# A transformer block on one core: the units without a dense product, and the row sums of the softmax, are put at another place in each chunk

## The chip, the cores and the metric

The kernel runs on one core of a Trainium2 chip. The metric is the device time of one execution in microseconds (us); three runs of the kernel before gave 5135.66, 5136.07 and 5133.8, median 5135.66. The profile shown below was taken of another execution, which took 5133.48 us.

## The reference, cut to what matters

The input x has 4 sequences of 2048 tokens with 512 features, float32. Each is normalised; then the result is x plus attention plus a feed-forward part:

```
xn  = layernorm(x)
qkv = xn @ qkv_w.T + qkv_b            # 16 heads of 32
att = softmax(q k^T / sqrt(32)) v     # over all 2048 keys
a   = att @ proj_w.T + proj_b
idx = top_2(xn[:, 0, :] @ Wr + br)    # two of 8 experts for a whole sequence
h   = gelu(xn @ W1[idx] + b1[idx])    # exact gelu
f   = (h @ W2[idx] + b2[idx]).sum(over the two) / 2
out = x + a + f
```

All matrix products are float32, except one small product described below.

## The kernel before, in words

**Units and chunks.** The attention is one long sequence of 1024 units. A unit is one tile of 128 keys against 512 queries of four heads (a group of heads). 16 units (kt = 0 to 15, NT = 16) make a chunk: one sequence b, one group of heads g, one block of queries qc. 4 chunks make a group, 4 groups a sequence, and there are 64 chunks, numbered here 0 to 63. The program is written out in one loop over U, the number of the unit, and every engine works through its own instructions in the order in which this loop issues them.

**What one unit issues.** On TensorE (PE): four small bf16 products that put minus the row maximum into four PSUM tiles (`shift`, L536, tiles s), the scores themselves on top (`score`, L544), and four score products of the unit 22 places ahead, of which only the maximum is wanted (`score_max`, L526, tiles m). ScalarE (ACT) takes the exponentials of the four s tiles (L656, into p). VectorE (DVE) takes the maxima of the four m tiles (L662). GpSimd (POOL) adds p to a running sum psum of the chunk (`add_weights`, L573 for the first and L575 for the others; not in the last chunk). Then, in even units, PE multiplies the p of the two units before with the values (`weigh`, L556, tile acc), which DVE adds up (L565). In odd units PE does one dense product of 32 matmul records (`product`, L395): a piece of a projection (kps, qps, vps, prps) or of the feed-forward part (hps, ops). So a pair of units does two sets of scores, one `weigh` and one dense product.

**Once per chunk.** After a chunk has ended, its psum is summed over the keys by a product with ones (`add_keys`, L581, tile keys), here in unit kt = 4 of the next chunk; ACT copies the result to SBUF (sums, L593). DVE takes the reciprocal in four parts in units 5, 7, 9 and 11 (L674), POOL multiplies in unit 12 (`divide`, L627) and SP stores the result two units later. In unit 13 PE transposes the maxima of a chunk ahead (`turn_maxima`, L618, tile mt), which DVE copies (L621); POOL has prepared them with five small instructions in unit 10 (L608, L610). In the last chunk there is no psum: `add_last` sums the p of two units by ones on PE, two units after them (16 matmul records).

**PSUM.** All these tiles come from one pool of eight banks (`ps`). A unit takes eight of them for its s and m tiles, and one more for acc or for the dense product; keys and mt each take one as well. A new tile goes into the bank that came free the longest ago, so a tile waits for the reader of an older tile.

**Who decides what a gap is.** `Plan` lays 496 dense products on 534 odd places (22 before unit 0, 512 after it), so 38 places have none: the gaps. Some products have fixed places (`fixed`: the k, q and v of the next group, L52 to L63); the feed-forward part and the output projection fill the rest in order. `rests` (L104 to L107) names the places where a gap is wanted, at kt = 13 of chosen chunks; 8 more are left over at the end of the list. A gap isn't put directly after the last w1 product of an expert, because the gelu stands there. Of the 38 gaps 29 lie at kt = 13, five at 15, two at 1 and two at 11: chunks 62 and 63 have four each (kt 1, 11, 13, 15), chunk 61 has two.

**Other things that a step below touches.** `root` (L342 to L347) takes the square root for the next sequence's normalisation in unit 1 of chunks 8, 24 and 40; its first instruction is a DVE operation on 128x16 numbers in SBUF (L343, sd<-mv). The buffers of p are four (`p_pool`): the exponentials of unit U + 4 wait until POOL has added unit U. The 32 gelus of ACT bring their tables with them. At the very end (L741 to L767) stand the last `weigh`, the last `add_last`, the projections of the last two blocks of queries and the stores.

Of the kernel before, what the change touches and what calls it, by code (L numbers as in the profile page):

```python
# [17 lines left out]
P = 128  # L18
# [12 lines left out]
class Plan:  # L31
# [6 lines left out]
    def __init__(self, B, DC, NCH, NT, TPC):  # L38
        self.per_group = NCH * NT
        self.per_seq = DC * self.per_group  # L40
        self.units = B * self.per_seq
        self.lead = NT + AHEAD
        self.items = {}
        self.extra = {}
        self.uses = []
        self.first_load = {}
        slots = list(range(-self.lead, 0)) + list(range(1, self.units, 2))

        fixed = {}
        for t in range(NT):  # L50
            fixed[slots[t]] = ("v", 0, t)
        for G in range(1, B * DC):  # L52
            b, g = divmod(G, DC)
            for c in range(NCH):
                if g:
                    at = [(G - 1) * self.per_group + 2 * (6 + 4 * c) + 1]
                    todo = [("k", b, g, c), ("q", b, g, c)]
                else:
                    at = [(G - 2) * self.per_group + 2 * (27 + (2 + TPC) * c) + 1]
                    todo = [("k", b, g, c), ("q", b, g, c)]  # L60
                    todo += [("v", b, c * TPC + i) for i in range(TPC)]
                for n, item in enumerate(todo):
                    fixed[at[0] + 2 * n] = item  # L63
        v_stored = {}
        for s, item in fixed.items():
            if item[0] == "v":
                v_stored[item[1], item[2] // TPC] = s + 3
        for b in range(B):
            for g in range(DC):
                for c in range(NCH):  # L70
                    self.first_load["v", (b, g, c)] = v_stored[b, c]
        for b in range(1, B):
            q1 = (b - 1) * self.per_seq + self.per_group
            q2 = q1 + self.per_group
            for n in range(NT):
                self.extra.setdefault(q1 + 2 * (16 + n) + 1, []).append(("stats", b, n))
                at = q2 + 2 * (1 + n + n // TPC) + 1
                self.extra.setdefault(at, []).append(("normal", b, n))
                self.extra.setdefault(at + 2, []).append(("turn", b, n))
            self.extra.setdefault(q2 + 1, []).append(("root", b, 0))  # L80
            for c in range(NCH):
                self.first_load[("xf", (b, c))] = self.first_load[("xq", (b, c))] = (
                    q2 + 2 * (2 + (TPC + 1) * c + TPC - 1) + 1 + 2
                )

        ffn = []
        for b in range(B):
            t0 = slots[0] if b == 0 else self.first_load[("xf", (b, 0))] + WARN
            for c in range(NCH):
                part = [("w1", b, c, k, f) for k in range(TOP_K) for f in range(DC)]  # L90
                part += [("w2", b, c, k, i) for k in range(TOP_K) for i in range(TPC)]
                ffn.append((t0, part))
        proj = []
        for b in range(B):
            for qc in range(NCH):
                if b == B - 1 and qc >= NCH - 2:
                    continue
                done = (b + 1) * self.per_seq - self.per_group + NT * (qc + 1) + 14
                self.first_load[("xl", ("at", b, qc))] = done + 1
                proj.append((done + 1 + WARN, [("proj", b, qc, i) for i in range(TPC)]))  # L100


        todo = len(fixed) + sum(len(p) for _, p in ffn + proj)
        spare = len(slots) - todo - 2 * TPC  # L104
        free = [s for s in slots if s > 0 and s not in fixed]
        rests = [s for s in free if s % NT == 13]
        rests = {rests[n * len(rests) // spare] for n in range(min(spare, len(rests)))}  # L107
        current, before, owed = [], None, 0
        for s in slots:
            if s in fixed:  # L110
                self.items[s] = [fixed.pop(s)]
                before = None
                continue
            curve = before is not None and before[0] == "w1" and before[4] == DC - 1
            before = None
            owed += s in rests
            if owed and not curve:
                owed -= 1
                continue
            if not current:  # L120
                for queue in (proj, ffn):
                    if queue and queue[0][0] <= s:
                        current = queue.pop(0)[1]
                        break
            if current:
                before = current.pop(0)
                self.items[s] = [before]
        assert not fixed and not proj and not ffn and not current, (proj, ffn, current)

        for s in slots:  # L130
            for it in self.items.get(s, []):
                for tag, key in self.needs(it):
                    self.uses.append((s, tag, key))
            for kind, b, n in self.extra.get(s, []):
                if kind in ("stats", "normal"):
                    self.uses.append((s, "xl", (kind, b, n // TPC)))
                elif kind == "turn":
                    self.uses.append((s, "xq", ("stage", b, n // TPC)))
        self.uses.append((self.units, "wb", ("proj",)))
        for u in range(2, self.units + 1, 2):  # L140
            kt, G = (u - 2) % NT, (u - 2) // self.per_group
            self.uses.append((u, "v", (*divmod(G, DC), kt // TPC)))
        self.uses.sort(key=lambda e: e[0])
        for s, tag, key in self.uses:
            if tag == "prow":
                self.first_load[tag, key] = 0
# [40 lines left out]
def block_kernel(  # L187
# [17 lines left out]
    B, N, D = x.shape  # L205
    E = Wr.shape[1]
    DC = D // P
    NT = N // P
    NCH = N // CH
    TPC = CH // P  # L210
    SCALE = float(HD) ** -0.5
    PSUM = bass.MemoryType.PSUM
    plan = Plan(B, DC, NCH, NT, TPC)
# [11 lines left out]
    def bank(name):  # L225
        return ps.tile([P, CH], F32, tag="bank", name=name)
# [284 lines left out]
    mx, negm, sacc, psums, sums, pT = {}, {}, {}, {}, {}, {}  # L511
    curves, waiting, ends = {}, {}, []
# [64 lines left out]
    def add_keys(where, ps, weights, again):  # L577

        for n, t in enumerate(weights):
            for j in range(GH):  # L580
                nc.tensor.matmul(  # L581
                    ps[rows_of(j), :], ones, t[:, j, :],
                    start=(n == 0), stop=(n == len(weights) - 1),
                )
        if again:
            nc.vector.tensor_tensor(sums[where], ps, sums[where], ALU.add)
        else:
            last = where == place(plan.units - 1)[:3]
            sums[where] = pair.tile(
                [P, CH], F32, tag="vrow" if last else "sums", bufs=2 if last else 1,  # L590
                name="sums_%d_%d_%d" % where,
            )
            nc.scalar.activation(sums[where], ps, AF.Identity)  # L593

    def add_last(u):
        add_keys(
            place(u)[:3], bank(f"keys_{u}"), [pT[u], pT[u + 1]], u > plan.units - NT
        )
# [37 lines left out]
    for U in range(-LEAD, plan.units):  # L636
        second = U >= 0
        first_pass = U + LEAD if U + LEAD < plan.units else None
        chunk, kt = divmod(U, NT)
        b, g, qc, _ = place(U) if second else (0, 0, 0, 0)  # L640
# [16 lines left out]
        curve = curves.pop(U, None)  # L657
# [6 lines left out]
        if first_pass is not None and last % NT == NT - 1:  # L664
            where, n = place(last)[:3], last // NT
# [3 lines left out]
        if last % NT == 0 and 0 < last <= plan.units:  # L669
            pending[0]()  # L670
        before = place(U - NT)[:3] if U >= NT else None
        if before is not None and kt in (5, 7, 9, 11):
            q = ts((kt - 5) // 2, P)
            nc.vector.reciprocal(sums[before][:, q], sums[before][:, q])  # L674
        if before is not None and kt == 12:
            divide(before)
            later(U + 2, lambda w=before: nc.sync.dma_start(
                att_dram[w[0], w[2]][:, w[1], :], att[w]))
# [6 lines left out]
        if second and U % 2 == 0:  # L685
            if U >= 2:
                weigh(U - 2)
            if U - 2 >= plan.units - NT:
                add_last(U - 2)
            if kt == 4 and before is not None:  # L690
                add_keys(before, bank("keys_%d_%d_%d" % before), [psums[before]], False)
        for step, sb, n in plan.extra.get(U, []):
            if step == "stats":
                if n == 0:
# [6 lines left out]
            else:  # L701
                c, i = divmod(n, TPC)
# [21 lines left out]
        for n, c in ((16, NCH - 1), (1, NCH - 2)):  # L724
            if U == plan.units - n:
# [7 lines left out]
                n = DC - 1 if c == NCH - 1 else DC  # L733
# [4 lines left out]
    U = plan.units  # L738
# [72 lines left out]
```

## Time and profile before

| | |
|---|---|
| median of 3 runs | 5135.66 us (5133.8 to 5136.07) |
| the profiled execution, its own time | 5133.48 us |
| its span, first to last instruction | 5131.6 us |
| PE busy | 5054.0 us (98%) |
| POOL busy | 4534.6 us (88%) |
| DVE busy | 3449.0 us (67%) |
| ACT busy | 2516.2 us (49%) |
| mean granted TensorE clock | 0.998 |

The time of an execution is 1.9 us above its span. Lines in the profile begin with the line of the kernel and the engine; then come the operation, the tile written and the tiles read (buffer numbers left out), how often, and in the table of groups the busy time, the mean of one in ns and the idle time ahead of it with what ended it. A line of the timeline has its start, its length, and in brackets the idle time of that engine before it with its releaser. A PE that the page calls busy isn't always at work: the records of matmuls that wait are drawn longer. The distance from the first shift product (L536) of a unit to that of the next is the length of the unit, and shows such waits.

Unit 0 starts at 160.1 us, chunk 62 at 4955.3, chunk 63 at 5016.3; the first product of the end (L746) starts at 5091.4.

### The profile page before, as it was taken

How to read it: one execution, taken by the hardware profiler on the slowest of the kernel's cores; microseconds unless marked ns; L12 is line 12 of the kernel's file. 1: busy time of each engine (PE TensorE's matmuls, PEld its weight loads, DVE VectorE, ACT ScalarE, POOL GpSimd, SP SyncE). 2: the span in 40 equal slices, each digit the busy share in tenths (PEclk: the TensorE clock that was granted, in tenths of full speed). 3: DMA queues.
4: the chain of work that ended last, by engine and by line, in shares of the span. 5: the costliest groups of instructions: out<-in, count | busy, mean ns of one | idle time of the engine just before them, and what ended most of it. 6: DMA issues, size and time to landing. Idle time of an engine off the chain costs nothing.

```text
span 5131.6 us, 108175 instructions
## 1 busy us (share of the span) xinstructions
PE 5054.0 (98%) x46020; PEld 1776.4 (35%) x46020; DVE 3449.0 (67%) x5495; ACT 2516.2 (49%) x4571; POOL 4534.6 (88%) x1430
## 2 busy tenths in 40 slices
PE   8999999999999999999999999999999999999998
PEld 2333333333333333333333333333333333333333
DVE  5666676766766667666766767766667666666672
ACT  1455545554544545554445454555444454555543
POOL 0699898989999999999999999989999999999992
PEclk9999999999999999999999999999999999999999
DMA  4211112201122112221121221221112211021112
GB/s 165 69 62 51 46 65 89 102 30 38 67 85 69 65 65 80 72 81 44 48 93 46 79 85 54 85 85 59 40 56 89 78 63 59 18 75 34 40 43 78
DMA packets 220675, 340.20 MB, mean 66 GB/s; under 512 B 14364, under 2 KB 129052, under 8 KB 205984
## 3 DMA queue, kind: packets, MB, share of 16 engines
q1 hardware_dynamic: 220192, 333.28, 19.2%
q8 instruction: 361, 5.91, 0.5%
q14 instruction: 122, 1.00, 0.1%
HBM read 249.61 MB, written 83.62 MB: 65 GB/s over the span
## 4 chain that ended last, share of the span: by engine, by line
PE 95%; POOL 2%; ACT 1%; DVE 0%; issue 0%; DMA 0%; SPq 0%; ACTq 0%; POOLq 0%
PE acc L556 18%; PE m L526 17%; PE s L544 17%; PE ops L395 9%; PE hps L395 9%; PE s L536 7%; PE kps L395 4%; PE vps L395 4%; PE qps L395 4%; PE prps L395 4%; POOL psum L575 2%; PE keys L581 1%; ACT L656 1%; PE xt L365 1%; ACT p L656 1%; PE mt L618 0%
## 5 line engine op out<-in xcount | busy, mean ns | idle before, releaser
L575 POOL TENSOR_TENSOR psum<-psum,p 128x2048 f32<-128x2048 f32 x882 | 4008.6, 4545 | 217.3 <-ACT p L656 182.1
L662 DVE TENSOR_REDUCE mx<-m 128x1 f32<-128x512 f32 x4096 | 2542.9, 683 | 1057.5 <-PE m L526 1056.9
L656 ACT ACTIVATE p<-s 128x512 f32<-128x512 f32 x4096 | 2118.1, 602 | 1797.3 <-PE m L526 1717.9
L544 PE MATMUL s<-qT,kT 32*128 32x512 f32 x8192 | 1924.0, 589 | 0.0
L526 PE MATMUL m<-kT,qT 32*128 32x512 f32 x8192 | 1908.4, 590 | 2.7 <-DMA wk<-in_qkv_wT_dram 1.5
L526 PEld LDWEIGHTS m<-kT,qT 32*128 32x128 f32 x8192 | 929.1, 184 | 325.3 <-issue 242.3
L556 PE MATMUL acc<-p,v 128*32 128x512 f32 x8192 | 990.0, 599 | 38.5 <-ACT p L656 38.5
L544 PEld LDWEIGHTS s<-qT,kT 32*128 32x128 f32 x8192 | 765.6, 186 | 31.0 <-issue 12.8
L556 PEld LDWEIGHTS acc<-p,v 128*32 128x32 f32 x8192 | 215.3, 109 | 738.5 <-ACT p L656 428.6
L395 PE MATMUL hps<-xf,w 128*32 128x512 f32 x4096 | 466.0, 595 | 0.2 <-ACT p L656 0.2
L395 PE MATMUL ops<-wb_w,h 128*32 128x512 f32 x4096 | 466.0, 595 | 0.2 <-ACT p L656 0.2
L536 PE MATMUL s<-negm,ones_b 32*128 32x512 bf16 x4096 | 421.4, 385 | 5.3 <-ACT p L656 3.5
L565 DVE TENSOR_TENSOR sacc<-acc,sacc 128x512 f32<-128x512 f32 x448 | 309.9, 692 | 154.7 <-PE acc L556 154.7
L536 PEld LDWEIGHTS <-ones_b 32*128 32x128 bf16 x4096 | 108.6, 91 | 842.3 <-issue 835.2
L573 POOL TENSOR_TENSOR psum<-p,p 128x2048 f32<-128x2048 f32 x63 | 286.1, 4541 | 117.6 <-ACT p L656 117.6
L407 ACT ACTIVATE h<-hps,b 128x512 f32<-128x512 f32 x115 | 79.0, 687 | 353.6 <-PE hps L395 353.6
L674 DVE RECIPROCAL sums<-sums 128x128 f32<-128x128 f32 x252 | 237.3, 942 | 0.7 <-ACT sums L593 0.7
L395 PE MATMUL vps<-wb_v,xq 128*32 128x512 f32 x2048 | 233.0, 595 | 2.3 <-issue 2.0
L395 PEld LDWEIGHTS ops<-wb_w,h 128*32 128x32 f32 x4096 | 120.0, 109 | 317.6 <-issue 229.8
L395 PEld LDWEIGHTS hps<-xf,w 128*32 128x32 f32 x4096 | 120.0, 109 | 317.1 <-issue 232.1
L395 PE MATMUL kps<-xq,wk 128*32 128x512 f32 x1920 | 218.4, 595 | 1.0 <-ACT p L656 0.2
L395 PE MATMUL qps<-xq,wq 128*32 128x512 f32 x1920 | 218.4, 595 | 0.1
(89 smaller groups left out, 1710.8 us busy)
## 6 DMA issues: line engine op xcount, KB each, us to landing
xq<-xn_dram SPq DMA_DIRECT2D x64, 1024.0 KB, 5.7
w<-in_W_dram SPq DMA_DIRECT2D x128, 256.0 KB, 3.1
xn_dram<-xq_stage SPq DMA_DIRECT2D x16, 1024.0 KB, 7.1
v_dram<-v SPq DMA_DIRECT2D x64, 256.0 KB, 2.4
xf<-xn_dram SPq DMA_DIRECT2D x16, 1024.0 KB, 6.1
v<-v_dram SPq DMA_DIRECT2D x64, 256.0 KB, 4.0
row<-in_x_dram SPq DMA_DIRECT2D x64, 256.0 KB, 5.9
part_dram<-row SPq DMA_DIRECT2D x64, 256.0 KB, 2.1
```

Source lines behind the costliest of these rows:

```text
L395: nc.tensor.matmul(pp[rows_of(j), :], lhsT[:, rows_of(j)], rhs, start=(first and n == 0), stop=(last and n == len(terms) - 1),)
L407: nc.scalar.activation(dst, src, AF.Identity, bias=col)
L526: nc.tensor.matmul(t, qT[b, g, qc][r, ts(i, P)], kT[b, g, kc][r, :], start=True, stop=True)
L536: nc.tensor.matmul(tiles[j], ones_b[r, :], negm[b, g, qc][r, :], start=True, stop=False)
L544: nc.tensor.matmul(tiles[j], kT[b, g, kt // TPC][r, ts(kt % TPC, P)], qT[b, g, qc][r, :], start=False, stop=True,)
L556: nc.tensor.matmul(acc[r, :], held["v", (b, g, kt // TPC)][:, (kt + n) % TPC, r], pT[u + n][:, j, :], start=(n == 0), stop=(n == 1),)
L565: nc.vector.tensor_tensor(t, acc, t, ALU.add)
L573: nc.gpsimd.tensor_tensor(psums[b, g, qc], pT[u - 1], pT[u], ALU.add)
L575: nc.gpsimd.tensor_tensor(psums[b, g, qc], psums[b, g, qc], pT[u], ALU.add)
L656: nc.scalar.activation(pT[U][:, j, :], tiles[j], AF.Exp, scale=SCALE)
L662: nc.vector.tensor_reduce(dst, t, AX.X, ALU.max, negate=True)
L674: nc.vector.reciprocal(sums[before][:, q], sums[before][:, q])
```

## The change

It does five things.

1. The wanted places of gaps are kt = 5 (not 13), spread evenly over the chunks with a running share, and only 4 places (not 8) are left over at the end. There are still 38 gaps: 34 at kt = 5 of chunks 1 to 62, and in chunk 63 kt = 1, 3, 13 and 15. The change calls this filling a third of the gaps at the end: chunks 61 to 63 have five gaps instead of ten.
2. In a chunk with a gap at kt = 5 the product of the ended chunk with ones (`add_keys`) is issued in unit 5 instead of 4; the reciprocals follow in units 7, 9, 11 and 13, `divide` in 14. In the 29 other chunks, the last one among them, nothing of this moves.
3. The fixed k and q products move by one odd place (from 13 and 15, 5 and 7, to 15 and 1, 7 and 9), so that place 5 is free.
4. In the last sequence the feed-forward part of the last two blocks of tokens is done in the other order; the output projection of a block may start two units later than before.
5. In the last chunk an `add_last`, which stands two units after the first of its two units, is issued one unit later still where that later unit is a gap.

The instructions of PE are the same in number (25,316 matmul instructions in both programs); SP has two DMAs more (the output projection falls between the pieces of a feed-forward part twice more, so one weight tile of 1 MB is loaded again twice).

```
-                    at = [(G - 1) * self.per_group + 2 * (6 + 4 * c) + 1]
+                    at = [(G - 1) * self.per_group + 2 * (7 + 4 * c) + 1]
...
-            for c in range(NCH):
+            order = list(range(NCH))
+            if b == B - 1:
+                order[NCH - 2 :] = order[: NCH - 3 : -1]
+            for c in order:
...
-                done = (b + 1) * self.per_seq - self.per_group + NT * (qc + 1) + 14
+                done = (b + 1) * self.per_seq - self.per_group + NT * (qc + 1) + 16
...
-        spare = len(slots) - todo - 2 * TPC
+        spare = len(slots) - todo - 4
         free = [s for s in slots if s > 0 and s not in fixed]
-        rests = [s for s in free if s % NT == 13]
-        rests = {rests[n * len(rests) // spare] for n in range(min(spare, len(rests)))}
+        rests = [s for s in free if s % NT == 5]
+        share = spare / len(rests)
...
-            owed += s in rests
-            if owed and not curve:
-                owed -= 1
-                continue
+            if s in rests:
+                owed += share
+                if owed > 0 and not curve:
+                    owed -= 1
+                    continue
...
+        self.keys_at = {}
+        for s in range(NT, self.units, NT):
+            ends = s + NT == self.units
+            self.keys_at[s // NT - 1] = 5 if s + 5 not in self.items and not ends else 4
...
-        if before is not None and kt in (5, 7, 9, 11):
-            q = ts((kt - 5) // 2, P)
+        keys = plan.keys_at.get(chunk - 1, 4)
+        part = (kt - keys - 1) // 2 if keys == 4 else (kt - keys - 2) // 2
+        if before is not None and kt % 2 and 0 <= part < TPC:
+            q = ts(part, P)
             nc.vector.reciprocal(sums[before][:, q], sums[before][:, q])
-        if before is not None and kt == 12:
+        if before is not None and kt == (12 if keys == 4 else 14):
             divide(before)
...
-            if U - 2 >= plan.units - NT:
-                add_last(U - 2)
-            if kt == 4 and before is not None:
-                add_keys(before, bank("keys_%d_%d_%d" % before), [psums[before]], False)
+        for u in (U - 2, U - 3):
+            late = u + 3 < plan.units and u + 3 not in plan.items
+            if u % 2 == 0 and u >= plan.units - NT and late == (u == U - 3):
+                add_last(u)
+        if before is not None and kt == keys:
+            add_keys(before, bank("keys_%d_%d_%d" % before), [psums[before]], False)
```

## The prediction on record

> **What bounds the kernel now.** I read the table of engines first, then the chain of waits, then the timeline of single units, each engine by itself, and last the waits of ACT at the end.
>
> ```profile
> PE 5054.0 (98%) x46020; PEld 1776.4 (35%) x46020; DVE 3449.0 (67%) x5495; ACT 2516.2 (49%) x4571; POOL 4534.6 (88%) x1430
> ...
> PE 95%; POOL 2%; ACT 1%; DVE 0%; issue 0%; DMA 0%; SPq 0%; ACTq 0%; POOLq 0%
> ```
>
> PE is the bound, and the chain runs on it for 95%; POOL has 2%, in chunks 61 and 62. So a change pays only by shortening PE's work or the waits between its products. The instructions of PE stay the same in number, so the whole answer is in the waits. They are seen in unit lengths, from first shift product (L536) to first shift product. The timeline of PE, a gap at unit 13 of chunk 10 and the pair after it:
>
> ```profile
> 1007.19 0.39 PE L536 MATMUL s<-negm,ones_b 32*128 32x512 bf16 x4
> ...
> 1009.24 0.40 PE L618 MATMUL mt<-ident_b,spread 128*128 128x128 bf16 x4
> 1009.67 0.86 PE L536 MATMUL s<-negm,ones_b 32*128 32x512 bf16 x4
> ...
> 1010.65 0.70 PE L526 MATMUL m<-kT,qT 32*128 32x512 f32 x2
> ...
> 1012.57 1.92 PE L556 MATMUL acc<-p,v 128*32 128x512 f32 x16
> 1014.42 0.39 PE L536 MATMUL s<-negm,ones_b 32*128 32x512 bf16 x4
> ...
> 1020.04 0.40 PE L536 MATMUL s<-negm,ones_b 32*128 32x512 bf16 x4
> ...
> 1023.94 0.39 PE L536 MATMUL s<-negm,ones_b 32*128 32x512 bf16 x4
> ```
>
> The normal pair takes 1023.94 - 1014.42 = 9.52: an odd unit with a product 5.61, an even one 3.90. The gap pair takes 14.42 - 7.19 = 7.23. Its work is only 1.99 (a bare odd unit, read at kt = 15) + 0.44 (mt: 6.05 against 5.61 in units 13 with a product) + 3.90 = 6.33; 0.90 is a wait. What it waits for is on ACT and DVE:
>
> ```profile
> 1008.53 2.06 ACT L656 ACTIVATE p<-s 128x512 f32<-128x512 f32 x4 [1.83 <-PE m L526]
> 1011.38 1.09 ACT L656 ACTIVATE p<-s 128x512 f32<-128x512 f32 x2 [0.78 <-PE s L544]
> ```
>
> The four exponentials end at 1010.59, 3.40 after the unit's start, and at 1010.65, or 3.46, the first m product of the next unit starts, into the bank just freed; what is queued behind it on PE waits as well. From there it is 1.92 to acc and 1.85 more to the next unit. ACT is then idle for 0.78.
>
> [...] A unit's s and m tiles fill all eight, so a unit without a product must wait for its predecessor's readers; the 0.90 above agrees. [...] it repeats here, 7.23 in 21 of the 27 gaps at kt = 13 up to chunk 61. [...]
>
> ```profile
> 783.42 4.28 DVE L343 TENSOR_SCALAR sd<-mv 128x16 f32<-128x16 f32 x1
> ...
> 2027.24 0.61 DVE L343 TENSOR_SCALAR sd<-mv 128x16 f32<-128x16 f32 x1
> ```
>
> In chunk 8 POOL's add had begun at 783.14 and ended at 787.67; in chunk 24 POOL was late and began at 2027.76.
>
> **The change part by part.**
>
> *Gaps up to chunk 61, before.* The 21 gap pairs above wait 0.90 each = 18.9. In six (chunks 6, 7, 22, 23, 38, 39) a stats step of DVE stands before the copy of mt, whose bank the next unit wants; the pair takes 7.94: 6 x 1.61 = 9.7. Three at kt = 15 wait 1.33 each, 4.0, one of them in chunk 62. Up to chunk 61 that is 31.3.
>
> *The same, after: 33 gaps at unit 5 with keys inside.* What keys costs on PE is seen in unit 4 now:
>
> ```profile
> 1042.85 1.04 PE L581 MATMUL keys<-psum,ones 128*32 128x512 f32 x8
> 1043.82 0.40 PE L536 MATMUL s<-negm,ones_b 32*128 32x512 bf16 x4
> ...
> 1043.95 0.60 ACT L593 ACTIVATE sums<-keys 128x512 f32<-128x512 f32 x1 [1.48 <-PE keys L581]
> ```
>
> 0.97 to the next unit; since unit 4 is 4.76 against 3.90, its net work is 0.86. In a gap it starts 2.04 after the unit's start, where mt starts now (1009.24), and the next shift comes at 3.0 instead of 2.48. The next m product still can't start before the exponentials end, at 3.46; from there 1.92 + 1.85 as above: again 7.23, but with 1.99 + 0.86 + 3.90 = 6.75 of work in it. The wait falls from 0.90 to 0.48. The 0.70 of the m product after a wait, against 0.59 otherwise, may go: then 0.38. I take 0.45; bounds 0.18 (only the change-over between kinds of products, 0.97 + 2.04 - 1.99 - 0.86 = 0.16) and 1.34 (keys not hidden at all). ACT's copy of keys fits: the exponentials end at 3.41, the next begin at 4.19, the copy takes 0.60. The stats step no longer matters, since ACT frees that bank. In chunks 8, 10, 24, 25 and 42 a transposition (0.59) lies in the gap too, and fills it: wait 0.1. Sum 28 x 0.45 + 5 x 0.1 = 13.1; saved 31.3 - 13.1 = 18.2. mt in unit 13 is now uncovered, 0.44; it is counted as work on both sides.
>
> *The lock.* In chunk 24 POOL's last add of the chunk before must end over 7.7 after its start for DVE to come first (8.2 now). Chunk 23 loses its gap but gets three additions of rows (L680, 1.3 each) late; I work out about 7.6. It costs nothing to 3.2, what unit 2 of chunk 8 waits now; I take 0.5.
>
> *Chunks 62, 63 and the end.* Before:
>
> ```profile
> 5017.96 2.06 ACT L656 ACTIVATE p<-s 128x512 f32<-128x512 f32 x4 [2.38 <-POOL psum L575]
> 5023.66 2.06 ACT L656 ACTIVATE p<-s 128x512 f32<-128x512 f32 x4 [3.64 <-POOL psum L575]
> ...
> 5019.11 18.36 POOL L575 TENSOR_TENSOR psum<-psum,p 128x2048 f32<-128x2048 f32 x4
> ```
>
> Four gaps make chunk 62 61.0 long, while POOL needs 15 x 4.6 for its adds; it ends at 5037.5, 21.2 into chunk 63, and the exponentials wait for p buffers. Work in chunk 62: 5 x 3.90 + 4 x 5.61 + 2.0 (gap) + 0.86 up to unit 9, then without m tiles (0.85 less each) 3 x 3.05 + 3 x 1.1 + 0.44: 57.7, wait 3.3. From chunk 63 to the first end product 75.1, with work 3.05 (unit 0) + 4 x 1.1 (gaps) + 10 x 4.77 (scores and a product, or `weigh` and `add_last`) + 5.6 (unit 4, with keys) = 60.75, and 3.6 for the last `weigh` and `add_last`: 64.35, wait 10.75. Together 14.05. After, chunk 62 has one gap and 69.1 of work; POOL starts its first add 7.4 into it and needs 15 x 4.6 + 1.3 (divide) + 1.3 (five small ones) = 71.6, so it ends about 10 to 11 into chunk 63. There unit 3's exponentials wait 1.0 for it, the gap at unit 1 costs 1.1, the gaps at 3, 13 and 15 are filled by `add_last` (1.72), the last exponential 0.5; with chunk 62's own gap 0.45: 3.05. Saved 11.0.
>
> *At nothing.* The moves with one answer: the k and q products only change places with others of the same 3.64. Reciprocals in 13 instead of 5: DVE there has 2.48 of maxima to 3.85, 0.94, 0.4 for mt, 0.8 with stats, all under the unit's 6.05; beyond that the next unit's m waits. `divide` and its store two units later: POOL is 1 to 2 us later after a gap (7.23 against two adds of 4.6), its adds then start 7 to 11 after their unit's start; the four p buffers allow about 15, then exponentials wait. The store stands ahead of all later loads on SP; POOL has two units (9.5) for it, and loads are issued 8 units ahead. The projection starts four units after its load, as now. Two more loads of 1 MB (6.9 each), 8 units (38 us) ahead. The 31 waits of 1.23 after gelus stay.
>
> *Sum.* 18.2 - 0.5 + 11.0 = 28.7 on a span of 5131.6: 5102.9. That execution took 5133.48, 2.2 under the median; I subtract from the median: 5135.66 - 28.7 = 5107.
>
> **Rivals.** (1) The forecast, with 0.38 to 0.48 per gap, lock 0 to 3.2, end within 3: 5102 to 5113. (2) Gaps filled nearly wholly, 0.18: 28 x 0.27 = 8 better, 5099. For it: keys delays the next unit until the banks are free but one. Against: that one, the last exponential at 3.41. (3) POOL still sets the pace at the end: its adds end 18 rather than 10 into chunk 63, so some 7 of the 11 stay, and the lock strikes in chunk 24, 2.7: 5117. For: POOL is the chain there now. Against: one gap instead of four. (4) Keys not hidden: 29 x 0.86 = 25 worse, 5132, no change. For: the wait is a chain through ACT, and keys adds a tile to it. Against: PE stands still while ACT works. (5) Slower: the copy of keys stands on ACT between the exponentials of units 5 and 6 and pushes the latter back, on top of (4): (0.86 + 0.60) x 34 = 50, 5157. It turns the sign from 28.7 / 34 = 0.84 per gap. For: ACT is in order. Against: 0.78 idle for 0.60, and the trace has psum ready 4 to 11 after a chunk's start, keys at 23. That the gaps don't move can't be: the plan is explicit.
>
> **Numbers.** Chances: (1) 0.60, (2) 0.13, (3) 0.16, (4) 0.06, (5) 0.05. A measurement can tell about 0.2% (10 us) from no change: faster 0.89, same 0.06, slower 0.05. Range 5097 to 5121, which leaves out (4), (5) and the tails.
>
> **What would show it.** A gap pair at kt 5 of 7.1 to 7.25, unit 4 there 3.90, gap chunks 74.3 (74.7 now), no difference by stats; L343 about 4.3 in chunks 8 and 40; chunk 63 near 63, its exponentials waiting for POOL under 3 in all. Wrong if the pairs take 8, if keys waits for psum, or if ACT waits for POOL in middle chunks.

## The result, and the profile after

The changed kernel takes 5114.66 us, the median of 6 runs (5110.6 to 5116.07); the kernel before 5135.05 us (5133.78 to 5136.07, 6 runs). The ratio is 0.996, with a 95% interval of 0.9947 to 0.9973: 20.4 us faster, where 28.7 were forecast. The profiled execution took 5115.77 us with a span of 5114.0.

The lines named below moved by 8: the shift product is L544 now, the exponentials L664, keys L589, the copy of keys L601, POOL's adds L581 and L583, the DVE operation of `root` L351. The table of engines, and the engines of the chain:

```profile
PE 5037.9 (99%) x46020; PEld 1763.7 (34%) x46020; DVE 3448.0 (67%) x5491; ACT 2515.2 (49%) x4576; POOL 4534.9 (89%) x1430
...
PE 2%; DVE 0%; ACT 0%; issue 0%
```

PE has the same 46020 records and is drawn 16.1 busy us shorter; its waits shrank, not its work. The chain could be followed back for 2% of the span only, so it is of no use here, and unit lengths must tell the rest. A gap at unit 5 of chunk 11, in the timeline of PE (units 4, 5, 6 and 7 begin with the shift lines):

```profile
1033.04 0.39 PE L544 MATMUL s<-negm,ones_b 32*128 32x512 bf16 x4
...
1036.94 0.39 PE L544 MATMUL s<-negm,ones_b 32*128 32x512 bf16 x4
...
1039.02 1.07 PE L589 MATMUL keys<-psum,ones 128*32 128x512 f32 x8
1040.02 0.40 PE L544 MATMUL s<-negm,ones_b 32*128 32x512 bf16 x4
...
1040.40 0.70 PE L534 MATMUL m<-kT,qT 32*128 32x512 f32 x2
...
1042.31 1.92 PE L564 MATMUL acc<-p,v 128*32 128x512 f32 x16
1044.17 0.40 PE L544 MATMUL s<-negm,ones_b 32*128 32x512 bf16 x4
```

Unit 4 takes 36.94 - 33.04 = 3.90 without keys; the gap pair takes 44.17 - 36.94 = 7.23 with keys in it. The first m product starts 40.40 - 36.94 = 3.46 after the gap's start, as before, and 1.91 and 1.86 follow. ACT in the same place:

```profile
1038.28 2.06 ACT L664 ACTIVATE p<-s 128x512 f32<-128x512 f32 x4 [1.83 <-PE m L534]
1040.20 0.63 ACT L601 ACTIVATE sums<-keys 128x512 f32<-128x512 f32 x1
1041.36 2.14 ACT L664 ACTIVATE p<-s 128x512 f32<-128x512 f32 x4 [0.53 <-PE s L552]
```

The copy stands exactly in ACT's idle stretch and still leaves 0.53 of it. The end, chunk 63 from 5007.08 on, on ACT and then on POOL:

```profile
5013.90 2.07 ACT L664 ACTIVATE p<-s 128x512 f32<-128x512 f32 x4 [0.38 <-POOL psum L583]
5018.51 2.06 ACT L664 ACTIVATE p<-s 128x512 f32<-128x512 f32 x4 [2.54 <-POOL psum L583]
```

```profile
5008.08 1.28 POOL L635 TENSOR_TENSOR att<-sacc,sums 128x512 f32<-128x512 f32 x1
5009.32 9.15 POOL L583 TENSOR_TENSOR psum<-psum,p 128x2048 f32<-128x2048 f32 x2
```

POOL's last add ends at 5018.47, 11.4 into chunk 63 instead of 21.2, and ACT waits 2.92 for it.

The other half of the result is in `root`, where an instruction of DVE lasts until an add of POOL that has begun before it is done (in chunk 8 of the changed kernel 779.62 to 783.90, beside POOL's 779.34 to 783.87); the prediction calls this the lock. L343 before, L351 now, each of the three executions during the attention (shortest, median and longest in ns):

```profile
L343 DVE TENSOR_SCALAR sd<-mv x3: 606/4278/4298, 783.4 to 3266.4; 128x16 f32<-128x16 f32 x3
```

```profile
L351 DVE TENSOR_SCALAR sd<-mv x3: 4277/4278/4279, 779.6 to 3247.8; 128x16 f32<-128x16 f32 x3
```

All three now take 4.28; the short one, in chunk 24, is gone. There POOL's first add began at 2016.42, and DVE's operation, at 2016.71, came second. And PE, in chunk 8 (timeline, then windows of 1 us: length, busy shares of PE, PEld, DVE, ACT and POOL, granted clock, share and rate of DMA):

```profile
784.78 1.12 PE L534 MATMUL m<-kT,qT 32*128 32x512 f32 x2 [1.20 <-ACT h L415]
786.69 3.26 PE L564 MATMUL acc<-p,v 128*32 128x512 f32 x16 [0.79 <-ACT p L664]
```

```profile
784.00:785.00 1.00, 0.22 (x1) 0.22 (x2) 0.82 (x3) 0.98 (x3) 0.40 (x2) 1.00 0.02 4
785.00:786.00 1.00, 0.90 (x2) 0.07 (x1) 1.00 (x2) 1.00 (x1) 0.08 (x1) 1.00 0.00 0
786.00:787.00 1.00, 0.31 (x4) 0.16 (x8) 0.76 (x2) 0.99 (x3) 0.00 (x0) 1.00 0.00 0
787.00:788.00 1.00, 1.00 (x9) 0.22 (x5) 0.00 (x0) 1.00 (x3) 0.00 (x0) 0.56 0.00 0
788.00:789.00 1.00, 1.00 (x12) 0.21 (x4) 0.00 (x0) 0.10 (x1) 0.82 (x1) 0.50 0.00 0
789.00:790.00 1.00, 1.00 (x12) 0.12 (x8) 0.00 (x0) 0.00 (x0) 1.00 (x1) 0.50 0.00 0
790.00:791.00 1.00, 1.00 (x12) 0.67 (x12) 0.69 (x1) 0.00 (x0) 1.00 (x1) 0.73 0.00 0
```

The sixteen acc products take 3.26 instead of 1.92: after the wait PE's clock was granted at half for 3.41 us. That happened after each of the three executions of L351, and in the kernel before only after the one in chunk 40. (The kernel before has one more such fall, in chunk 63 at 5024.2, which the changed one has not.) A mean clock of 0.998 hides it.

### The profile page after: what moved, and what is told of

The parts are those of the page before. It is cut to its first block, busy times and chain, and to the rows that moved or that the text cites. A ratio compares the mean times of both kernels' runs of the same rounds, so it can differ in the third digit from the quotient of the medians.

```text
span 5114.0 us, 108163 instructions
## 1 busy us (share of the span) xinstructions
PE 5037.9 (99%) x46020; PEld 1763.7 (34%) x46020; DVE 3448.0 (67%) x5491; ACT 2515.2 (49%) x4576; POOL 4534.9 (89%) x1430
## 5 line engine op out<-in xcount | busy, mean ns | idle before, releaser
L583 POOL TENSOR_TENSOR psum<-psum,p 128x2048 f32<-128x2048 f32 x882 | 4008.1, 4544 | 193.3 <-ACT p L664 152.7
L664 ACT ACTIVATE p<-s 128x512 f32<-128x512 f32 x4096 | 2117.1, 603 | 1817.2 <-PE m L534 1729.7
L544 PE MATMUL s<-negm,ones_b 32*128 32x512 bf16 x4096 | 404.8, 385 | 2.0 <-ACT p L664 1.8
L544 PEld LDWEIGHTS <-ones_b 32*128 32x128 bf16 x4096 | 103.0, 91 | 857.5 <-issue 857.5
L581 POOL TENSOR_TENSOR psum<-p,p 128x2048 f32<-128x2048 f32 x63 | 286.0, 4540 | 119.4 <-ACT p L664 119.4
```

The costliest lines, as they stand in the source:

```text
L544: nc.tensor.matmul(tiles[j], ones_b[r, :], negm[b, g, qc][r, :], start=True, stop=False)
L581: nc.gpsimd.tensor_tensor(psums[b, g, qc], pT[u - 1], pT[u], ALU.add)
L583: nc.gpsimd.tensor_tensor(psums[b, g, qc], psums[b, g, qc], pT[u], ALU.add)
L664: nc.scalar.activation(pT[U][:, j, :], tiles[j], AF.Exp, scale=SCALE)
```

## The experiments

In each comparison "wait" is the length of a unit less its work, with the prediction's prices of work. The theory to be tested (A): a gap pair is as long as its chain of exponentials, 7.23, whatever small work lies in it, so keys is paid for by time that was idle; and the lock in `root` took back a part of that. Rivals: the place of the gaps rather than keys brought the gain, or the end of the program did (C); or the lock's stalls only show a delay that would be there anyway (B).

### e1_root_on_act_after: the changed kernel without the DVE operation

The small constant is added by ACT inside the square root, so the DVE operation is gone and nothing can be locked there.

```
+    eps = const.tile([P, 1], F32, name="eps")
+    nc.gpsimd.memset(eps, EPS)
-        nc.vector.tensor_scalar(sd[:np_, a:z], mv[:np_, a:z, 1], EPS, None, ALU.add)
-        nc.scalar.activation(sd[:np_, a:z], sd[:np_, a:z], AF.Sqrt)
+        nc.scalar.activation(sd[:np_, a:z], mv[:np_, a:z, 1], AF.Sqrt, bias=eps[:np_])
```

> The changed kernel with one thing taken away: in root the small DVE addition of epsilon on 128x16 (sd<-mv) is gone, ScalarE adds it as the bias of its square root. Theory A (the shortfall against the forecast is the lock): DVE's small operation waited 4.3 us behind GpSimd's add in chunks 8, 24 and 40, PE stood idle and ran at half clock for 3.4 us afterwards; unit 2 of those chunks waits 4.5, 4.2 and 4.9 us now and will wait under 0.5 us each, so some 13 us less than the changed kernel: 5101 us. Rival B (the two table loads of 1.28 us each around the square root make the wait, the lock lies beside them): unit 2 still waits 3 us or more, 5111 us or above.

Measured: 5104.73 us (5102.71 to 5105.05, 5 runs), ratio to the kernel before 0.9941 (0.9927 to 0.9954); the changed kernel stands at 0.996, so this is about 10 us less. ACT in chunk 8:

```profile
779.05 1.28 ACT L353 ACT_TABLE_LOAD   x1
780.35 0.31 ACT L353 ACTIVATE sd<-mv,eps 128x16 f32<-128x16 f32 x1
...
782.57 1.28 ACT L665 ACT_TABLE_LOAD   x1 [0.50 <-PE m L535]
```

```profile
784.51 1.92 PE L565 MATMUL acc<-p,v 128*32 128x512 f32 x16 [1.16 <-ACT p L665]
```

The waits of units 2 and 3 in chunks 8, 24 and 40 fall from 13.9 in all to 3.7, 1.23 in each; under 0.5 was expected, without the table loads of 1.28 on ACT that stay. No half clock is left before the end of the program. 13.9 - 3.7 = 10.2 is about what the times show. A holds in the main, B falls. This is the fastest version in the study.

### e2_root_on_act_before: the same edit on the kernel before

```
-        nc.vector.tensor_scalar(sd[:np_, a:z], mv[:np_, a:z, 1], EPS, None, ALU.add)
-        nc.scalar.activation(sd[:np_, a:z], sd[:np_, a:z], AF.Sqrt)
+        nc.scalar.activation(sd[:np_, a:z], mv[:np_, a:z, 1], AF.Sqrt, bias=eps[:np_])
```

> The kernel before with the same edit. Theory A: there the lock struck only in chunks 8 and 40 (3.2 and 2.9 us beyond the gelu's 1.2), so about 6 us less: 5129 us, and the difference between the two kernels without the lock is about 28 us, near the forecast of 28.7. Rival B: no change, 5135 us.

Measured: 5131.44 us (13 runs) beside 5135.84, ratio 0.9993 (0.9985 to 1.0002), an interval that touches no change. The profile gives the size: the same units fall from 8.7 to 5.0, 3.7 us, of which 1.66 is the half clock in chunk 40. So the lock and its clock cost 3.7 before and 10.2 after: 6.5 us of the change's gain were lost there. Without them the change brings 5131.44 - 5104.73 = 26.7, where about 28 was expected. The 1.66 may not belong to the lock: in chunk 40 a wait of 2.56 stays without it, and only the fall of the clock is gone.

### e3_keys_in_4: the gaps stay at unit 5, keys goes back to unit 4

```
-            self.keys_at[s // NT - 1] = 5 if s + 5 not in self.items and not ends else 4
+            self.keys_at[s // NT - 1] = 4
```

> The changed kernel with the sums over keys always in unit 4, so that the 34 gaps at unit 5 are empty; reciprocals and division follow at their old units. Theory A (the gap pair is timed by the last exponential and takes 7.23 us whatever lies in it, up to 0.48 us more): the pair still takes 7.2 us, unit 4 goes from 3.90 to 4.76, so about 0.86 x 29 and a little for the five gaps with a transposition: 27 us more than the changed kernel, 5142 us. Rival C (keys is not hidden in the gap, the gain comes from the end and from where the gaps lie): within 5 us of the changed kernel.

Measured: 5144.92 us (5143.69 to 5147.76, 13 runs), ratio 1.002 (1.0012 to 1.0028): 30 us above the changed kernel and slower than the kernel before. A gap of this kernel in the timeline of PE:

```profile
1042.76 1.04 PE L589 MATMUL keys<-psum,ones 128*32 128x512 f32 x8
1043.73 0.40 PE L544 MATMUL s<-negm,ones_b 32*128 32x512 bf16 x4
...
1045.72 1.09 PE L544 MATMUL s<-negm,ones_b 32*128 32x512 bf16 x4
...
1050.95 0.40 PE L544 MATMUL s<-negm,ones_b 32*128 32x512 bf16 x4
```

The pair is 50.95 - 43.73 = 7.22 with nothing in it; unit 4 pays its 0.86 again. 34 x 0.86 = 29.2; the five pairs with a transposition take 8.22 instead of 7.67, 2.8 more; the half clock struck once instead of three times, 3.3 less. That makes 28.7, and the profiles are 28.8 apart. So the gain is keys, not the place of the gaps; C falls for this part.

### e4_keys_twice: the product of keys is computed twice in a gap

```
+            ps_ = bank("keys_%d_%d_%d" % before)
+            if keys == 5:
+                for j in range(GH):
+                    nc.tensor.matmul(
+                        ps_[rows_of(j), :], ones, psums[before][:, j, :], start=True, stop=True
+                    )
-            add_keys(before, bank("keys_%d_%d_%d" % before), [psums[before]], False)
+            add_keys(before, ps_, [psums[before]], False)
```

> The changed kernel with the product of keys computed twice in the 33 or 34 gaps at unit 5, the second result kept. Theory A: of the 0.86 us more per gap 0.32 us fill the wait that is left (0.48 less the 0.16 of change-over), so the pair goes from 7.23 to 7.77 us and the kernel is 28 x 0.54 + 5 x 0.75 = 19 us slower, 5134 us. If nothing of the wait can be filled: 29 us slower, 5144 us. If the wait were longer than the unit lengths show: under 10 us slower.

Measured: 5131.96 us (5131.04 to 5134.39, 12 runs), ratio 0.9995 (0.9986 to 1.0003), 17.3 above the changed kernel.

```profile
1038.98 0.39 PE L544 MATMUL s<-negm,ones_b 32*128 32x512 bf16 x4
...
1041.06 1.07 PE L706 MATMUL keys<-psum,ones 128*32 128x512 f32 x8
1041.92 1.07 PE L589 MATMUL keys<-psum,ones 128*32 128x512 f32 x8
1042.92 0.39 PE L544 MATMUL s<-negm,ones_b 32*128 32x512 bf16 x4
...
1046.82 0.39 PE L544 MATMUL s<-negm,ones_b 32*128 32x512 bf16 x4
```

The pair is 46.82 - 38.98 = 7.84: of the second 0.86 only 0.25 hides, 0.61 shows. 29 x 0.61 and 0.75 in each of the five gaps with a transposition make 21.4; in this profile the half clock struck once instead of three times, 3.3 less, and unit 0 starts 2.5 earlier: 15.6, as far as the two profiles are apart. Unit 6 now has its plain 3.90, and the wait that stays, 0.23, lies in unit 5: it is the floor of a gap.

### e6_gaps_in_13: the gaps of the changed kernel put back at 13

The number of gaps up to chunk 62 and the end stay as in the changed kernel, and keys is in unit 4.

```
-        rests = [s for s in free if s % NT == 5]
+        rests = [s for s in free if s % NT == 13]
...
-            self.keys_at[s // NT - 1] = 5 if s + 5 not in self.items and not ends else 4
+            self.keys_at[s // NT - 1] = 4
```

> The changed kernel with its 34 gaps at kt = 13 instead of 5 and the sums over keys always in unit 4: the same end of the program, the same number of gaps, but the transposition of the maxima in the gap as in the kernel before. Theory A: a gap chunk takes 74.7 instead of 74.26 us, three gaps with a stats step 0.7 more, the five gaps with a turned block no longer gain: 34 x 0.43 + 3 x 0.7 = 17 us slower than the changed kernel, 5131 us; so of the gain two thirds is the content of the gaps and the rest, some 4 us net of the lock, the end. Rival C (the end makes the gain): within 5 us of the changed kernel.

Measured: 5127.22 us (5126.56 to 5129.85, 20 runs), ratio 0.9986 (0.998 to 0.9993). The gap pairs are 7.23 with mt (0.44) in them, save three beside stats (7.94), three with a transposition (7.74) and one of 7.51. Between this and the changed kernel lie 12.6 us, between this and the kernel before some 7 us. The expected 17 is there, but not alone: the gaps up to chunk 61 wait 31.9 against 14.9 in the changed kernel, 17.0 more, and the end takes 1.4 more; the units of `root` wait 4.7 less, since the clock fell once instead of three times and in chunk 24 DVE came first. By its profile the end saves 10.0 against the kernel before (177.2 from chunk 62 on, with three dense products of 3.62 more in it, against 176.3), and the units before chunk 62 wait 3.4 longer. So keys in the gap are worth some 17 us, the end 10 to 11, and `root` takes part of it back.

### e7_sums_by_dve: DVE copies keys in the chunks with a gap

```
-            nc.scalar.activation(sums[where], ps, AF.Identity)
+            if plan.keys_at.get(where[0] * 16 + where[1] * 4 + where[2], 4) == 5:
+                nc.vector.tensor_copy(sums[where], ps)
+            else:
+                nc.scalar.activation(sums[where], ps, AF.Identity)
```

> The changed kernel with the copy of keys out of PSUM on VectorE instead of ScalarE where the keys lie in a gap. If ScalarE's copy cost PE something in a gap (the rival of the forecast: it pushes the next exponentials back), this is faster. Theory A: ScalarE has 0.78 us idle there and the copy 0.60, so nothing is to be gained; VectorE is at its maxima to 3.85 us after the unit's start and frees the bank at about 4.5, 0.2 to 0.3 us later than the next product wants it, and 0.7 to 0.9 later in the four gaps with a stats step: 6 to 10 us slower, 5121 to 5125 us.

Measured: 5120.35 us (5118.73 to 5121.9, 7 runs), ratio 0.9971 (0.996 to 0.9982), 5.7 above the changed kernel. DVE in a gap (unit 5 starts at 1036.32):

```profile
1037.68 2.48 DVE L673 TENSOR_REDUCE mx<-m 128x1 f32<-128x512 f32 x4 [0.54 <-PE m L534]
1040.08 0.68 DVE L602 COPY sums<-keys 128x512 f32<-128x512 f32 x1
1040.93 2.48 DVE L673 TENSOR_REDUCE mx<-m 128x1 f32<-128x512 f32 x4 [0.17 <-PE m L534]
```

Behind four maxima the copy ends 4.44 after the gap's start; ACT's ended at 3.89. The pair grows from 7.23 to 7.41, and 34 x 0.18 = 6.1. No cost of the copy is seen on ACT, and on DVE it has one: of the two, ACT's idle stretch is the better place, the reverse of rival (5).

### e8_scores_first: the last 0.25

In the lock-free kernel, unit 6 behind a gap does its four score products ahead of the four m products, so that they don't queue behind the one that waits.

```
+        split_order = kt == 6 and plan.keys_at.get(chunk - 1, 4) == 5
+        if split_order:
+            score(U, range(GH), tiles)
         for h in range(2):
-            if second:
+            if second and not split_order:
```

> Two edits on the changed kernel: the lock taken away as in the other run, and in unit 6 after a gap the four score products with their exponentials stand ahead of the four whose maxima are wanted, so that the products that wait for the bank of the last exponential come 0.86 us later and no longer wait. Theory A: the pair falls from 7.23 to about 6.9 us (6.75 of work and 0.16 of change-over), 28 x 0.32 = 9 us, on top of 13 us for the lock: 5093 us. If the wait comes back elsewhere (VectorE gets its first m tile 0.86 us later and the next unit waits for it): no better than without the lock alone, 5101 us.

Measured: 5108.42 us (5108.06 to 5109.73, 5 runs), ratio 0.9948 (0.9935 to 0.9962): not the 5093 of the theory, nor a gain over e1. The timeline of PE:

```profile
1032.22 0.39 PE L545 MATMUL s<-negm,ones_b 32*128 32x512 bf16 x4
...
1035.30 0.39 PE L545 MATMUL s<-negm,ones_b 32*128 32x512 bf16 x4
...
1039.20 0.40 PE L545 MATMUL s<-negm,ones_b 32*128 32x512 bf16 x4
...
1041.63 3.64 PE L404 MATMUL kps<-xq,wk 128*32 128x512 f32 x32
```

```profile
1037.45 2.48 DVE L674 TENSOR_REDUCE mx<-m 128x1 f32<-128x512 f32 x4 [1.38 <-PE m L535]
1039.85 0.68 DVE L574 TENSOR_TENSOR sacc<-acc,sacc 128x512 f32<-128x512 f32 x1
1040.56 2.48 DVE L674 TENSOR_REDUCE mx<-m 128x1 f32<-128x512 f32 x4
```

The pair falls to 39.20 - 32.22 = 6.98, as the theory wanted. But the maxima start 2.15 after unit 6, against 1.54 in the changed kernel, the addition of acc stands behind them, and the maxima of unit 7 begin only when DVE has done both; PE's m products in unit 7 wait for their banks, and the dense product starts 2.43 after that unit's start instead of 1.99. Unit 7 waits 0.40, where 0.25 was saved: 34 x 0.15 = 5.1, and the two profiles stand 5.3 apart from unit 0 on. The times alone, whose intervals overlap, would not tell the two kernels apart. The wait was given back by the next engine.

### e5_add_last_not_late: the last part of the change undone

```
-            late = u + 3 < plan.units and u + 3 not in plan.items
+            late = False
```

> The changed kernel with add_last always two units after its first unit, so that the gaps of the last chunk at 3, 13 and 15 are empty. Theory A: PE waits for the exponentials of the gap units instead, about 1 us each at 13 and 15: the stretch from the start of chunk 63 to the first product of the end grows by 1 to 3 us. If add_last in the gaps gives nothing: no change of that stretch.

Measured: one run, 5116.61 us. By the profile, the stretch from the start of chunk 63 to the first product of the end takes 67.5 against 66.5 in the changed kernel, 0.9 more before rounding and just under the 1 to 3 expected; from chunk 62's start to the end it is 5114.8 - 4938.3 = 176.5 against 175.9: 0.6 us. So by this single profile, moving `add_last` into the gaps of chunk 63 is worth half a microsecond to one. The rest of the gain at the end probably lies in having one gap instead of four in chunk 62; that is not shown, since neither this nor the other order of the feed-forward part was tried alone.

## Why the prediction was right, and where it was not

The time lies in the range, and in the forecast's mechanism; it is 7.7 above the number. In the profiled spans 17.6 were saved, not 28.7. Step by step:

**Gaps up to chunk 61: right.** The pair was worked out as 7.23 and is 7.23; the wait is 0.48 where 0.45 was taken. One small term was too low: a gap with a transposition waits 0.33, not 0.1, since a floor of 0.23 stays (e4), a little above the 0.16 of the change-over. The 33 gaps wait 14.9 in all, forecast 13.1: 1.8 missed. The stats steps make no difference, as forecast. The contents of a gap side by side:

| in the gap | kernel | work of the pair | pair | wait |
|---|---|---|---|---|
| nothing | e3 | 5.89 | 7.22 | 1.33 |
| mt | before, e6 | 6.33 | 7.23 | 0.90 |
| keys | changed | 6.75 | 7.23 | 0.48 |
| keys and a transposition | changed | 7.34 | 7.67 | 0.33 |
| keys twice | e4 | 7.61 | 7.84 | 0.23 |
| a transposition alone | e3 | 6.48 | 8.22 | 1.74 |

The last row is not timed by the exponentials: in chunk 10 of e3, DVE copies the transposed tile only from 971.09 to 971.72, after a reciprocal of 0.94, and two m products, released by it, start at 971.77. Small work is free only while its own reader is in time.

**"The lock": the step that failed.** It took 0.5, in chunk 24 alone, with 3.2 as its upper end; it was 6.5 (10.2 after less 3.7 before, e1 and e2). Two terms were missing. The first is where the lock strikes. In chunk 24 POOL came first by 0.28 us, and that cost 1.35; the prediction's own working, 7.6 where over 7.7 was needed, already had it so, and the 0.5 was too little for it. But it also struck in chunk 40, where the kernel before had the same 4.3 and lost 0.04 by it (2.60 with it, 2.56 without, in e2), and the changed one 1.94. ACT in chunk 40, before and then after, shows the reason:

```profile
3267.38 1.91 ACT L660 ACTIVATE h<-h 128x2048 f32<-128x2048 f32 x1
...
3270.76 0.22 ACT L344 ACTIVATE sd<-sd 128x16 f32<-128x16 f32 x1 [0.17 <-DVE sd L343]
```

```profile
3252.16 0.22 ACT L352 ACTIVATE sd<-sd 128x16 f32<-128x16 f32 x1 [3.37 <-DVE sd L351]
```

Before, a gelu (L660) stood on ACT ahead of the square root, and ACT was busy until DVE had nearly done; the change moved that gelu to another unit, and ACT waits 3.37 for DVE. I had taken chunks 8 and 40 as unchanged because the operation's length was. Chunks 24 and 40 together make 3.3. The second term is PE's clock, 1.65 each time and three times instead of once, 3.3 more; it stood in no row that I had priced.

**The clock.** The same wait occurs with and without it. Units 2 and 3 of chunk 8 wait 3.18 in the kernel before and in e3, and 4.82 in the changed kernel, e4, e5 and e6, where the clock fell; chunk 40 waits 3.17 in four kernels and 4.82 to 4.87 in two; chunk 24 waits 2.60 in e3 and e4, 4.22 in the changed kernel, and 5.86 in e5, where the half clock lasted twice as long, 6.83. Each 3.41 us at half clock costs 1.65. e3 in chunk 8, with the same two idle times of PE as the changed kernel:

```profile
789.54 1.12 PE L534 MATMUL m<-kT,qT 32*128 32x512 f32 x2 [1.20 <-ACT h L415]
791.45 1.92 PE L564 MATMUL acc<-p,v 128*32 128x512 f32 x16 [0.79 <-ACT p L664]
```

What differs is where the wait falls on a grid that the clock's own changes show. In each of the eight profiles with such falls, the clock falls and rises whole numbers of 3.413 us apart: in the changed kernel it falls at 787.13, 2022.75 and 3254.97, which are 362 and 361 steps. Chunk 8 laid on that grid, in the changed kernel and then in e3 (columns as in the windows above, but busy times in us):

```profile
783.72:787.13 3.41, 1.56 (x6) 0.45 (x10) 2.76 (x6) 3.17 (x6) 0.63 (x3) 1.00 0.05 16
787.13:790.54 3.41, 3.41 (x24) 1.01 (x20) 0.48 (x1) 0.97 (x2) 2.36 (x1) 0.50 0.00 0
```

```profile
786.77:790.18 3.41, 2.21 (x16) 0.68 (x8) 3.13 (x4) 1.46 (x3) 2.35 (x3) 1.00 0.26 77
790.18:793.60 3.42, 2.63 (x26) 0.70 (x28) 1.44 (x4) 2.67 (x5) 0.65 (x1) 1.00 0.00 0
```

In the changed kernel the wait lies in one window, of which PE is drawn busy for 0.46, and the next window runs at half clock. In e3 the same wait is split over two, 0.65 and 0.77 busy, and nothing follows. Behind `root` the clock fell eleven times in seven profiles, after windows of 0.42 to 0.62. Nine waits of over 2 us there went unpunished: eight of them have no window under 0.65, the ninth (chunk 40 of e2) has one of 0.58. So in these profiles it is mostly the place on the grid that decides, though the drawn share does not part all the cases. The forecast could have had it as a bound only.

**Chunks 62, 63 and the end: right.** From chunk 62's start to the end 175.9, against 176.3, with three more dense products in it (3 x 3.62, the difference of an odd unit with a product and a bare one): 11.3 saved, forecast 11.0. From chunk 63 to the first end product it took 66.5; the sum had 64.35 + 2.6. The "near 63" of the last paragraph is that sum without the 3.6 of the last `weigh` and `add_last`; the last `weigh` starts 63.0 after chunk 63 does. ACT waited 2.92 for POOL, forecast under 3. The fall of the clock in chunk 63 that only the kernel before has lies in the wait that was saved; what it cost there is not separated.

**The beginning.** Unit 0 starts at 162.5, not 160.1, and nothing there was changed. In ten profiles it starts at 160.0 to 160.5 four times and at 162.4 to 162.9 six times, with either kind of plan (e2, on the kernel before, 162.9; e4 160.0). The 2.4 is chance between executions, and a single pair of profiles carries it; its cause is open. The 62 runs of the kernel before beside the experiments fall into two groups about as far apart: 29 took 5133.4 to 5134.6, 33 took 5135.5 to 5136.8.

**The sum.** Waits worked out unit by unit, with the prediction's prices, give all of the 17.6: 16.3 saved in the gaps up to chunk 61 (forecast 18.2) and 11.3 from chunk 62 on (11.0), less 5.2 in the units of `root` (8.7 to 13.9; forecast 0.5), 2.4 in the other units (forecast nothing) and 2.4 at the beginning. The 5.2 is less than 6.5, because the gelu's wait in chunk 40 was among the 8.7 and is now, with 1.2, among the other units.

**The rivals.** Gaps filled nearly wholly (2): no, the floor is 0.23 and the chain 7.23. POOL at the end (3): no, though its second half, the lock in chunk 24, came. Keys not hidden (4) and the copy in the way (5): no; e3 and e7 show the reverse.

## What to carry to other kernels

Before filling an idle place, find what its length is set by: here a chain of exponentials makes 7.23 with 0, 0.44 or 0.86 us of small work in it, so about 1.1 us is free (an estimate: 7.23 - 5.89 and the floor of 0.23) and the next is not; and only if the reader of that work is in time. Reordering a schedule moves which instructions of DVE and GpSimd meet (here an operation of 4.28 us that took 0.16 when it came first, in e6), and a rare step (three in this kernel) can take back a quarter of the gain (6.5 of 26.7): price every such meeting in each place, with what else stands on the waiting engine there, not only the one that visibly changes, and remove its cause where that is as cheap as a bias in an activation (ACT's square root takes 0.31 us with it in e1, 0.22 without). Compare unit lengths, not the sum of busy time, and hold one engine's saved wait against the next engine's queue (e8).

## What the runs showed of the hardware

PE's clock fell to half for 3.41 us, once for 6.83 (chunk 24 of e5), after waits in which PE was not idle throughout: the window ahead of the fall in chunk 8 has it drawn busy for 0.46, and the eleven behind `root` lie between 0.42 and 0.62. In chunk 63 of the kernel before and of e2 the clock fell after windows of 0.19 and 0.20, and in each of the ten profiles it is at half for the last 10 to 14 us. The changes of the clock lie on a grid of 3.413 us (362 and 361 steps between the three falls of the changed kernel), and the wait of chunk 8 was punished where it lay in one window of the grid, 0.46 busy, and not where it was split over two, 0.65 and 0.77 busy (e3). How little of a window PE must be busy for the clock to fall is open: a window of 0.62 was followed by a fall and one of 0.58 was not (chunk 40 of e2), and records of matmuls that wait are drawn longer (four shift products 1.09 in the gap of e3, 0.40 elsewhere).

In the seven profiles that have it, the DVE operation on 128x16 numbers ran 21 times during the attention. 19 times it starts 0.28 to 0.29 after an add of POOL, and takes 4.27 to 4.30: it ends within 0.03 of the add's end. Twice it comes just ahead of the next add: it takes 0.16 in e6, and 0.61 in chunk 24 of the kernel before, where it ends with the add that went before. So in these 21 runs of it the operation lasts until what POOL had begun is done, and which of the two begins first decides between 0.16 and 4.30 us.
